# Four small reorderings in a four-layer graph kernel: fetch order, row copies, and VectorE's place in the unit

## The chip, the cores and the metric

The kernel runs on one NeuronCore of a Trainium2 chip. The metric is device time in microseconds (us) of one launch, the median of three runs. The profile is of one further execution, and its span (first to last instruction) is a little shorter than that execution's time.

## The reference, cut to what matters

There are 64 graphs of 256 nodes with 256 features, and one sparse adjacency matrix `adj` (256 x 256, self loops included) that all graphs share. Layers 0, 1 and 3 are the same function with different weights; layer 2 is an attention layer.

```python
def gnn(h, A):                                   # layers 0, 1 and 3
    pre_u = einsum('bud,dk->buk', h, W1[:d]); pre_v = einsum('bvd,dk->bvk', h, W1[d:])
    hidden = relu(pre_u[:, :, None] + pre_v[:, None] + b1)          # for every pair (u, v)
    S = sigmoid(einsum('buvk,ko->buvo', hidden, W2)[..., 0] + b2)   # one score for every pair
    a = einsum('buv,bud->bvd', S * A, h)
    m = einsum('uv,bud->bvd', A, h) * h
    return beta1 * h + beta2 * (a @ Wa + ba) + beta3 * (m @ Wm + bm)
def attention(x, A):                             # layer 2
    f = x @ W1.T; f1 = f @ W2 + b2
    c = softmax(leaky_relu(f1[:, :, None] + f1[:, None, :]) + A)
    return c @ f + bias2 + x
```

Only pairs with an edge need a score, because S is multiplied by A.

## The kernel before, in words

**Edges instead of pairs.** Once, before the loop, the kernel sorts the edges into 16 tiles of 128 edges and one rest tile of 64 edges (for two graphs it fills 128 partitions). A tile lies between 64 nodes u and 64 nodes v. The score of an edge needs row u of pre_u plus row v of pre_v for that edge. Two graphs are worked on at once, so a gathered tile holds 128 edges x 2 graphs x 256 features.

**Two ways of gathering rows.** Eight tiles (`FAST`) are made on TensorE: ScalarE copies rows of `pu` and `pv` into `pre` (`rows_u` copies two tiles at a time, `rows_v` one), and a matmul with a one-hot matrix `pick` spreads them to edges in PSUM (tile `ga`). The other eight (`FETCHED`) and the rest tile are fetched by DMA: SyncE writes `pu` and `pv` to DRAM tables (`tableu`, `tablev`, one write for each half m of the nodes), and GpSimd issues two indirect DMAs for each tile, the first a **copying** fetch from `tableu`, the second an **adding** fetch from `tablev` that accumulates on the first. `FETCHES` is the order of these, as pairs (tile, 0 for copying or 1 for adding); tile -1 is the rest tile `left`. The adding fetch of a tile must wait until its copying fetch has landed. The order of all fetches on GpSimd's queue is fixed by `issue_after(fetches[-1])`. `fetch(st, AHEAD)` issues the first six as soon as the first half of the tables has been handed to SyncE; those read only that half. In two of the six kinds of units two tiles more are fetched and two fewer are made (`FETCHES_MORE`).

**Scores.** For each gathered tile and graph VectorE does one fused relu, multiply and sum (`rated`, output `junk`, sum in a column of `raw`). When the columns of the first half (`EARLY`: rest tile, self loops, tiles with m = 0) are there, `rated_all(EARLY, 0)` makes ScalarE take the tanh (`val`) and VectorE four products (`rm`), and `early` starts the matrix `sa` = S * A from the rest tile and the diagonal (matmuls ps<-ro,guo, then four `sa` operations on VectorE). `rated_all(LATE, 1)` does the same for m = 1 at the end of the unit. `spread` then turns `rm` into `sa` with 32 small matmuls (ps<-rm,gu), the first sixteen with the EARLY `rm`, the other sixteen with the LATE one.

**Units.** Two streams, a and b, each take two graphs at a time, and sixteen such pairs pass through each. A unit is one call of `beside(heavy, light, placed)`: the heavy part is the scores of one stream, the light part what the other stream does between its scores and its next ones: `spread` and `finish` of the layer before, attention where it comes, `before` of the next layer (pre_u, pre_v, tables, first row copies) and the matmuls adj x h. The light part is a generator, and what it yields, (p, f), says how many steps of made tiles and of fetched tiles are traced at that place. Those numbers are `STEPS` and `beside` (a dict of the same name inside `before`). `halfway` mixes `finish` of the last layer with `before` of the next pair's layer 0. One **round** of six units serves two graphs of each stream:

| unit | heavy: scores of | light: the other stream's work | `placed` |
|---|---|---|---|
| U1 | a, layer 0 | b: end of the last layer, then `before` of layer 0 | no |
| U2 | b, layer 0 | a: end of layer 0, `before` of layer 1 | yes |
| U3 | a, layer 1 | b: end of layer 0, `before` of layer 1 | yes |
| U4 | b, layer 1 (more fetched tiles) | a: end of layer 1, attention, `before` of the last layer | no |
| U5 | a, last layer (more fetched tiles) | b: end of layer 1, attention, `before` of the last layer | no |
| U6 | b, last layer | a: end of the last layer, then `before` of layer 0 | no |

So the fetches that serve the scores of U2 are started near the end of U1, and so on: each unit has its own **fetch stream**.

**Who sets the order.** A scheduler orders each engine's instructions; `tc.issue_after(x)` fixes that what is inside comes after x on x's engine. With `placed`, `stay` puts the scores of fetched tiles, the diagonal's scores and the EARLY tanh behind what was traced last on their engine, so that VectorE meets them where the program has them; EARLY is then done as soon as four made tiles are traced and the first four fetched tiles and the rest tile are scored. Without it all made tiles are traced first, EARLY comes near the end, and the scheduler is free. Nearly every instruction is recorded under line 79 (the wrapper that remembers the last one), fetches under line 824, table writes under 677.

Of the kernel before, what the change touches and what calls it, by code (L numbers as in the profile page):

```python
# [17 lines left out]
GNN = ("L0_gnn_", "L1_gnn_", "L3_gnn_")  # L18
LAST = GNN[2]
# [18 lines left out]

FETCHES = [(0, 0), (1, 0), (2, 0), (0, 1), (3, 0), (1, 1)]
FETCHES += [(-1, 0), (2, 1), (4, 0), (3, 1), (-1, 1), (5, 0), (6, 0), (4, 1), (7, 0), (5, 1), (6, 1), (7, 1)]  # L40
FETCHES_MORE = FETCHES[:-2] + [(8, 0), (6, 1), (9, 0), (7, 1), (8, 1), (9, 1)]

AHEAD = 6

STEPS = {
    GNN[0]: [(1, 1), (1, 1), (0, 1), (1, 0), (0, 1), (2, 1)],
    GNN[1]: [0, 0, 0, (0, 1), (0, 1), 1],
    LAST: [1, 1, (0, 1), (1, 1), (0, 1), (2, 1)],
}

VEC = {}
# [11 lines left out]
def blk(c):  # L63
    return slice(c * P, (c + 1) * P)
# [37 lines left out]
def adj_seq_kernel(ctx: ExitStack, tc: tile.TileContext, a: dict, out: bass.AP):  # L102
# [15 lines left out]
    tensor, vector, scalar = Noting(nc.tensor), Noting(nc.vector), Noting(nc.scalar)  # L118
# [383 lines left out]
    def few(stack):  # L502
# [139 lines left out]
        def more(st, l):  # L642

            return (st["side"], l) in (("a", LAST), ("b", GNN[1]))

        def before(st, l):

            hT = st["hT"]
            pu = one.tile([P, 2, 2, D], FP, tag="pu" + st["side"], name="pu")
            pv = one.tile([P, 2, 2, D], FP, tag="pv" + st["side"], name="pv")  # L650
            pre = one.tile([P, len(FAST), 2 * D], FP, tag="pre" + st["side"], name="pre")
            order = [(m, g) for m in range(2) for g in range(2)]
            if l == LAST:
                order = [(m, g) for g in range(2) for m in range(2)]

            beside = {LAST: [0, (0, 1), (0, 1), (0, 1)], GNN[1]: [0] + [(0, 1)] * 3, GNN[0]: [0, 0, (0, 2), (0, 1)]}[l]
            beside = dict(zip(order, beside))
            st["tables"] = [
                tables.tile([N, 2 * D], FP, tag="table" + t + st["side"], name="table" + t) for t in "uv"
            ]  # L660

            st["pu"], st["pv"], st["pre"] = pu, pv, pre
            if l != GNN[1]:
                st["own"] = one.tile([P, 2, 2, D], FP, tag="own", name="own")
            t = one.tile([P, FIRST, 2, D], FP, tag="fetched" + st["side"], name="fetched")
            st["fetched"] = [t[:, f] for f in range(FIRST)]
            for m, g in order:
                if l == LAST and (m, g) == (1, 0):
                    st["flip"](1)
                t = psum()  # L670
                for c in range(2):
                    mm(out=t, lhsT=hT[:, c, g, blk(m)], rhs=w1[l][:, c], start=c == 0, stop=c == 1)
                scalar.copy(pu[:, m, g, :], t[:, 0, :])
                vector.tensor_tensor(pv[:, m, g, :], t[:, 1, :], b1row[l], ALU.add)
                if g == 1:
                    for rows, x in zip(st["tables"], (pu, pv)):
                        nc.sync.dma_start(out=rows[blk(m)], in_=flat(x)[:, m])
                    if m == 0:
                        st["fetches"] = list(FETCHES_MORE if more(st, l) else FETCHES)

                        if numbered:
                            fetch(st, AHEAD)
                if l != GNN[1]:
                    vector.tensor_tensor(st["own"][:, m, g, :], t[:, 0, :], pv[:, m, g, :], ALU.add)
                if g == 1:
                    if m == 0:
                        rows_u(st, 0, 2, 0, 0)
                    rows_v(st, 4 - 4 * m, 2, 0)
                yield beside[(m, g)]
                if l == GNN[1] and (m, g) == (0, 1):  # L690
                    st["turn"](0)
                    yield 0, 1
                    st["turn"](1)
                    yield 0
            yield REST_OF_IT

            yield from mixed(st, l, later if past else None, (0,) if more(st, l) else (0, 1))

        def scores(st, l, placed):
# [3 lines left out]


            stay = behind if placed else lambda engine: nullcontext()
            pre = st["pre"]
            raw = wk.tile([P, LATE.stop], FP, tag="raw", name="raw")
            val = wk.tile([P, LATE.stop], FP, tag="val", name="val")
# [21 lines left out]
            fetched = st["fetched"]  # L730
            fetch(st, len(FETCHES_MORE))

            def tile_scores(t, k, m, i):
                col = BLOCKS + 16 * m + 4 * k + i
                both(t, col, col + 8)
# [18 lines left out]
            def itself(m):  # L754

                with stay(vector):
                    if l == GNN[1]:
                        vector.tensor_tensor(*(flat(t)[:, m] for t in (own, st["pu"], st["pv"])), ALU.add)
                    both(own[:, m], DIAGONAL + 2 * m, DIAGONAL + 2 * m + 1)

            def made():
                for n, (k, m, i) in enumerate(fast):
                    t = ga.tile([P, 2, D], FP, tag="ga", name="ga")
                    with stay(tensor):
                        mm(out=t, lhsT=pick[:, k, 4 * m + i, :], rhs=pre[:, n], start=True, stop=True)
                    tile_scores(t, k, m, i)
                    if 2 * n + 2 < len(fast):

                        with tc.issue_after(past[-1]) if past else nullcontext():
                            rows_u(st, 2 * n + 2, 2, *FAST[2 * n + 2][:2])  # L770
                            if n != 1:
                                rows_v(st, 2 * n + 2, 2, FAST[2 * n + 2][0])
                    if n in (1, 2) and not placed:
                        itself(n - 1)
                    count.append(n)
                    yield
                    if n == 2 and more(st, l):
                        yield from mixed(st, l, None, (1,), ga)

            def got(made):  # L780
                for f, block in enumerate(blocks):
                    if f == FIRST:
                        if placed:
                            while len(count) < 4:
                                next(made)
                        else:
                            for _ in made:
                                yield
                        with stay(vector):
                            rated(left, REST)  # L790
                        rated_all(EARLY, 0)
                        yield
                        if placed:
                            early(st)
                            yield
                    if f < 2 and placed:
                        itself(f)
                    with stay(vector):
                        tile_scores(fetched[f], *block)
                    if f == FIRST + 1 and not placed:  # L800
                        early(st)
                    yield
# [27 lines left out]
        def rows_u(st, f, n, k, m):  # L830

            h = halves[k]
            scalar.copy(
                st["pre"][h, f : f + n],
                st["pu"][h, m].rearrange("p g d -> p (g d)").unsqueeze(1).to_broadcast([64, n, 2 * D]),
            )

        def rows_v(st, f, n, k):

            for n in range(f, f + n):  # L840
                i = FAST[n][2]
                scalar.copy(
                    st["pre"][halves[1 - k], n], st["pv"][halves[i % 2], i // 2].rearrange("p g d -> p (g d)")
                )
# [32 lines left out]
        def after(st, l):  # L877
            yield 1
            yield from spread(st, l)
            yield from finish(st, l)  # L880

        def stream(side, starts):

            sts = [{"b": b, "side": side} for b in starts]
            load(sts[0])
            short = [before(sts[0], GNN[0])]
            for i, st in enumerate(sts):
                yield short, (st, GNN[0]), False
                yield [after(st, GNN[0]), before(st, GNN[1])], (st, GNN[1]), True
                yield [after(st, GNN[1]), attention(st), before(st, GNN[2])], (st, GNN[2]), False  # L890
                short = [after(st, GNN[2])]
                if i + 1 < len(sts):
                    load(sts[i + 1])
                    short = [halfway(after(st, GNN[2]), 4, before(sts[i + 1], GNN[0]), 2)]
            yield short, None, False
# [29 lines left out]
        past, numbered, fetches, later = [], [], [], []  # L925
# [119 lines left out]
```

## Time and profile before

| | us |
|---|---|
| median of three runs | 3469.57 (3468.32 to 3470.26) |
| the profiled execution's own time | 3468.32 |
| its span | 3466.6 |
| TensorE busy | 3361.7 (97%) |
| VectorE busy | 2639.6 (76%) |
| GpSimd busy | 2416.1 (70%) |
| ScalarE busy | 1557.2 (45%) |
| granted TensorE clock, mean | 0.991 |

A busy TensorE is not a TensorE at its peak, because matmuls overlap and their ends are modelled: a stall inside a group shows as a longer interval from one start to the next. One round takes about 210 us, and the sixteen rounds are alike, so stalls are read from the timeline of one round. A GpSimd row is the issue of a fetch, not its transfer. "Idle" in front of a row names what ended the wait.

### The profile page before, as it was taken

The page shows a single profiled execution, that of the slowest core. Times are in us where ns is not written, and L with a number is a line of the kernel's source. Part 1 is how long each engine was busy: PE and PEld are TensorE (multiplying, and loading weights), DVE is VectorE, ACT ScalarE, POOL GpSimd, SP SyncE. Part 2 cuts the span into 40 slices and gives each one's busy share as a digit, 9 for nine tenths or more (in the row PEclk, how much of TensorE's full clock was granted, in tenths as well). Part 3 has the DMA queues.
Part 4 walks back from the last instruction along what each step waited for, and adds up shares of the span by engine and source line. Part 5 has one row for each costly group of instructions (what it writes and reads, how often), then busy time and mean ns, then how long its engine had stood idle before and what let it go on. Part 6 is the DMA issues. An engine that isn't in the chain of part 4 may idle for free.

```text
span 3466.6 us, 48384 instructions
## 1 busy us (share of the span) xinstructions
PE 3361.7 (97%) x14200; PEld 2067.6 (60%) x14200; DVE 2639.6 (76%) x10523; ACT 1557.2 (45%) x2833; POOL 2416.1 (70%) x1882
## 2 busy tenths in 40 slices
PE   6999999999999999999999999999999999999998
PEld 3566565565656566565665656656565665656655
DVE  5777787777777777777777877777777777777776
ACT  2444444444444444444444444444444444444442
POOL 3767777677767767677677776777767676776765
PEclk7999999999999999999999999999999999999999
DMA  5788787877878778787787877878787787877875
GB/s 148 164 185 188 166 207 164 193 176 178 197 168 196 179 178 186 176 196 171 178 188 165 197 170 187 183 170 205 167 196 173 178 197 165 193 179 175 190 162 129
DMA packets 289070, 620.81 MB, mean 179 GB/s; under 512 B 39072, under 2 KB 56352, under 8 KB 288800
## 3 DMA queue, kind: packets, MB, share of 16 engines
q0 software_dynamic: 204800, 461.49, 65.2%
q1 hardware_dynamic: 82416, 154.96, 12.8%
q8 instruction: 115, 1.88, 0.2%
q10 hardware_dynamic: 1584, 1.20, 0.1%
q14 instruction: 155, 1.27, 0.1%
HBM read 500.06 MB, written 117.44 MB: 178 GB/s over the span
## 4 chain that ended last, share of the span: by engine, by line
PE 68%; POOL 9%; DMA 7%; issue 7%; DVE 6%; ACT 3%; ACTq 0%; POOLq 0%; DVEq 0%
PE ps L79 52%; PE ga L79 16%; POOL fetched L824 8%; DMA fetched<-tablev,ids_v 4%; DVE junk L79 3%; ACT pre L79 2%; DMA fetched<-tableu,ids_u 2%; DVE rm L79 1%; DMA tableu<-pu 1%; POOL left L824 1%; DVE sa L79 1%; ACT val L79 1%; ACT pu L79 1%; DVE own L79 0%; DVE pv L79 0%
## 5 line engine op out<-in xcount | busy, mean ns | idle before, releaser
L824 POOL DMA_INDIRECT fetched<-tablev,ids_v x832 | 1317.3, 1583 | 381.1 <-issue 257.0
L824 POOL DMA_INDIRECT fetched<-tableu,ids_u x832 | 843.7, 1014 | 547.1 <-DMA tableu<-pu 286.7
L79 DVE SCALAR_TENSOR_TENSOR junk<-fetched,L_gnn_w2row 128x256 f32<-128x256 f32 x1664 | 643.0, 419 | 171.3 <-DMA fetched<-tablev,ids_v 167.3
L79 PE MATMUL ga<-pre,pick 128*128 128x512 f32 x1408 | 723.5, 609 | 37.0 <-ACT pre L79 27.4
L79 PE MATMUL ps<-L_gnn_w,hT 128*128 128x512 f32 x1536 | 708.0, 598 | 5.7 <-DMA hT<-in_xT_dram 5.7
L79 DVE SCALAR_TENSOR_TENSOR junk<-ga,L_gnn_w2row 128x256 f32<-128x256 f32 x1408 | 538.3, 419 | 103.7 <-PE ga L79 92.2
L79 PEld LDWEIGHTS ps<-L_gnn_w,hT 128*128 128x128 f32 x1536 | 280.6, 191 | 323.7 <-issue 300.2
L79 ACT COPY pre<-pv 64x512 f32<-64x512 f32 x704 | 434.0, 616 | 72.6 <-DVE pv L79 49.3
L79 PE MATMUL ps<-sa,h 128*128 128x256 f32 x1536 | 363.7, 382 | 13.2 <-DVE sa L79 8.9
L79 PEld LDWEIGHTS ps<-sa,h 128*128 128x128 f32 x1536 | 292.5, 191 | 126.0 <-issue 68.5
L79 ACT COPY pre<-pu 64x1024 f32<-64x1024 f32 x352 | 361.6, 1044 | 8.0 <-DVE ids_v L79 0.6
L79 PEld LDWEIGHTS ga<-pre,pick 128*128 128x128 f32 x1408 | 249.2, 191 | 184.4 <-issue 91.3
L79 ACT COPY pu<-ps 128x256 f32<-128x256 f32 x384 | 142.8, 372 | 481.3 <-PE ps L79 430.8
L79 ACT ACTIVATE hb<-hT,L_gnn_zbias,scas 128x512 f32<-128x512 f32 x128 | 97.3, 807 | 477.9 <-DVE hT L79 354.5
L79 DVE TENSOR_TENSOR rm<-gva,val 128x256 f32<-128x256 f32 x768 | 280.1, 420 | 33.1 <-ACT val L79 24.2
L79 PE MATMUL ps<-adj,h 128*128 128x256 f32 x1280 | 297.2, 384 | 4.0 <-issue 4.0
L79 PEld LDWEIGHTS ps<-adj,h 128*128 128x128 f32 x1280 | 242.1, 191 | 73.7 <-issue 40.3
L79 DVE TENSOR_TENSOR pv<-ps,L_gnn_b1row 128x256 f32<-128x256 f32 x384 | 161.7, 421 | 134.5 <-ACT pu L79 125.6
L79 PEld LDWEIGHTS ps<-rm,gu 128*64 128x64 f32 x3072 | 175.1, 138 | 135.2 <-issue 50.3
L79 ACT COPY aT<-ps 128x512 f32<-128x512 f32 x192 | 112.4, 585 | 315.9 <-PE ps L79 284.6
L79 PE MATMUL ps<-rm,gu 128*64 128x128 f32 x3072 | 218.7, 281 | 23.0 <-DVE rm L79 22.6
L79 PE MATMUL ps<-aT,L_gnn_Wa 128*128 128x512 f32 x512 | 240.6, 592 | 0.0
(149 smaller groups left out, 4211.8 us busy)
## 6 DMA issues: line engine op xcount, KB each, us to landing
tableu<-pu SPq DMA_DIRECT2D x192, 256.0 KB
tablev<-pv SPq DMA_DIRECT2D x192, 256.0 KB
hT<-in_xT_dram SPq DMA_DIRECT2D x32, 512.0 KB
h<-in_x_dram SPq DMA_DIRECT2D x64, 256.0 KB
out_dram<-h SPq DMA_DIRECT2D x64, 256.0 KB
fetched<-tableu,ids_u POOLq DMA_INDIRECT x832
fetched<-tablev,ids_v POOLq DMA_INDIRECT x832
L_gnn_w<-in_L_gnn_W_dram SPq DMA_DIRECT2D x6, 256.0 KB
```

What stands on the lines that cost most here:

```text
L79: self.last = getattr(self.engine, op)(*a, **k)
L824: this = nc.gpsimd.indirect_dma_start(out=to, out_offset=None, in_=rows, in_offset=bass.IndirectOffsetOnAxis(ap=ids, axis=0), compute_op=( ...
```

## The change

It does five things.

1. `APART` is a second order of fetches, in which a copying fetch follows another copying fetch only at the very start. It is used in the streams of U2, U3, U4 and U5 (in the last two through `FETCHES_MORE`). The streams of U6 and U1 (`tight`) keep `FETCHES`.
2. The row copies of later made tiles (`rows_u`, `rows_v` from tile 2 on) are queued on ScalarE behind the last row copy of `before`, which fills tiles 0 and 1.
3. U1 and U6 become `placed` (from the second round on), which moves EARLY, `early` and the rest tile's score to the middle of the unit and fixes VectorE's order there. The diagonal's scores (`itself`) stay where they were in all units, through `diagonal_later`.
4. `STEPS[LAST]` moves one fetched tile's step from the first z matmuls to one step earlier.
5. The dict `beside` of layer 0 spreads four fetched steps evenly over the four blocks of `before`.

```diff
-FETCHES_MORE = FETCHES[:-2] + [(8, 0), (6, 1), (9, 0), (7, 1), (8, 1), (9, 1)]
+APART = [(0, 0), (1, 0), (0, 1), (2, 0), (1, 1), (3, 0)]
+APART += [(-1, 0), (2, 1), (4, 0), (3, 1), (5, 0), (-1, 1), (6, 0), (4, 1), (7, 0), (5, 1), (6, 1), (7, 1)]
+FETCHES_MORE = APART[:-2] + [(8, 0), (6, 1), (9, 0), (7, 1), (8, 1), (9, 1)]
...
-    LAST: [1, 1, (0, 1), (1, 1), (0, 1), (2, 1)],
+    LAST: [1, (1, 1), 0, (1, 1), (0, 1), (2, 1)],
...
-            beside = {LAST: [0, (0, 1), (0, 1), (0, 1)], GNN[1]: [0] + [(0, 1)] * 3, GNN[0]: [0, 0, (0, 2), (0, 1)]}[l]
+            beside = {LAST: [0, (0, 1), (0, 1), (0, 1)], GNN[1]: [0] + [(0, 1)] * 3, GNN[0]: [(0, 1)] * 4}[l]
...
-                        st["fetches"] = list(FETCHES_MORE if more(st, l) else FETCHES)
+                        tight = (st["side"], l) in (("b", LAST), ("a", GNN[0]))
+                        st["fetches"] = list(FETCHES_MORE if more(st, l) else FETCHES if tight else APART)
...
                     rows_v(st, 4 - 4 * m, 2, 0)
+                    st["rows"] = scalar.last.ins
...
+            diagonal_later = placed and (st["side"], l) in (("b", GNN[0]), ("a", GNN[1]))
...
-                        with tc.issue_after(past[-1]) if past else nullcontext():
+                        with tc.issue_after(past[-1]) if past else nullcontext(), tc.issue_after(st["rows"]):
...
-                    if n in (1, 2) and not placed:
+                    if n in (1, 2) and not diagonal_later:
...
-                    if f < 2 and placed:
+                    if f < 2 and diagonal_later:
...
-                yield short, (st, GNN[0]), False
+                yield short, (st, GNN[0]), i > 0
```

The order before, for comparison:

```python
FETCHES = [(0, 0), (1, 0), (2, 0), (0, 1), (3, 0), (1, 1)]
FETCHES += [(-1, 0), (2, 1), (4, 0), (3, 1), (-1, 1), (5, 0), (6, 0), (4, 1), (7, 0), (5, 1), (6, 1), (7, 1)]
```

## The prediction

> **What bounds the kernel now.** I read the page first: busy shares, then its costliest groups.
>
> ```profile
> PE 3361.7 (97%) x14200; PEld 2067.6 (60%) x14200; DVE 2639.6 (76%) x10523; ACT 1557.2 (45%) x2833; POOL 2416.1 (70%) x1882
> ...
> L824 POOL DMA_INDIRECT fetched<-tablev,ids_v x832 | 1317.3, 1583 | 381.1 <-issue 257.0
> L824 POOL DMA_INDIRECT fetched<-tableu,ids_u x832 | 843.7, 1014 | 547.1 <-DMA tableu<-pu 286.7
> ```
>
> TensorE is the bound, and the change takes no matmul away: only TensorE's stalls can be won or lost. 97% busy hides some, since a stalled matmul counts as busy, so I took intervals between starts in the trace. A run of 32 ps<-rm,gu takes 1.90 us unstalled; 2 ga<-pre,pick take 0.86. Against such values a round of about 210.7 us holds some 9 us of stalls, nearly all at the six unit boundaries. The timeline shows them. U4's end:
>
> ```profile
> 1253.56 1.04 ACT L79 COPY pre<-pu 64x1024 f32<-64x1024 f32 x1
> ...
> 1254.25 1.09 DVE L79 TENSOR_TENSOR rm<-gva,val 128x256 f32<-128x256 f32 x3
> 1254.63 2.52 ACT L79 COPY pre<-pv 64x512 f32<-64x512 f32 x4
> ...
> 1255.30 1.12 PE L79 MATMUL ga<-pre,pick 128*128 128x512 f32 x2 [1.01 <-ACT pre L79]
> ```
>
> ScalarE copies rows of tiles 2 and 3 (1.04 us) before the last rows of tile 0, and TensorE, in order, waits 1.01 us for tile 0. U1's end:
>
> ```profile
> 1360.35 0.31 ACT L79 ACTIVATE val<-raw,L_gnn_halfb 128x16 f32<-128x16 f32 x1 [2.71 <-DVE junk L79]
> ...
> 1360.94 1.49 DVE L79 TENSOR_TENSOR rm<-gva,val 128x256 f32<-128x256 f32 x4 [0.62 <-ACT val L79]
> ...
> 1362.15 1.42 PE L79 MATMUL ps<-rm,gu 128*64 128x128 f32 x16 [0.55 <-DVE rm L79]
> ```
>
> Here the LATE `rm` comes last: the group of 32 took 2.88 us in nearly every round, 0.98 over. U6's end is alike (0.61 over). At U3's end the wait reaches back to a fetch:
>
> ```profile
> 791.90 0.42 DVE L79 SCALAR_TENSOR_TENSOR junk<-fetched,L_gnn_w2row 128x256 f32<-128x256 f32 x1 [1.28 <-DMA fetched<-tablev,ids_v]
> ...
> 794.78 1.33 PE L79 MATMUL ps<-rm,gu 128*64 128x128 f32 x16 [1.30 <-DVE rm L79]
> ```
>
> And GpSimd's queue at the start of a stream (here U4's):
>
> ```profile
> 1420.77 0.98 POOL L824 DMA_INDIRECT fetched<-tableu,ids_u  x1 [3.17 <-DMA tableu<-pu]
> 1422.05 1.13 POOL L824 DMA_INDIRECT fetched<-tableu,ids_u  x1 [0.30 <-issue]
> 1423.49 0.96 POOL L824 DMA_INDIRECT fetched<-tableu,ids_u  x1 [0.30 <-issue]
> 1425.84 1.56 POOL L824 DMA_INDIRECT fetched<-tablev,ids_v  x1 [1.38 <-issue]
> ```
>
> Three copying fetches at 0.98 + 0.30 = 1.28 us each, then the first adding fetch, 5.07 us after the stream's start. Over 95 streams that distance was 3.9 to 7.1 us, and three issues need 3.84: almost always the queue already waits, after the third copying fetch, for the first to land. The first fetch's gap says what started the stream: 3 to 6 us of waiting for tableu in the streams of U3 to U6, but 0.30 in those of U1 and U2, in every round: there GpSimd goes from stream to stream without a pause.
>
> **What the Trainium skill says.** "Perfetto Trace Analysis", section "DMA Instruction — SWDGE (GPSIMD)": a fetch's row on GpSimd ends with its descriptors, not with its data. The trace agrees: rows of 1.55 us, but the packets of a stream's last adding fetch end 4.4 to 7.1 us after its issue. "DMA: Bandwidth & Descriptors", section "Why a DMA increments its semaphore by 16 and not by 1": data is there when all engines have counted. In the stream at 1324.08 the counts of the first copying fetch came from 1328.38 to 1329.90, and the adding fetch went at 1330.16. The same page, section "Two DMAs through the same engine are not ordered": within a queue of an engine descriptors start in order. So a later copying fetch shouldn't delay an earlier one's landing; the ends that the trace has for the three, staggered (1329.90, 1330.52, 1331.15), agree.
>
> **The change, part by part** (per round).
>
> *Row copies ahead.* Queued behind tiles 0 and 1, the 1.04 us copy no longer precedes tile 0. At U4's end ga could start at about 1254.3 instead of 1255.30; the second half of ps<-rm,gu then needs the `rm` that ends at 1255.34, against 1256.35 now. Gain **0.9**. U5's end has the same order (TensorE 0.48 over), but what follows is paced by the fetch chain below, so I count it there. The other boundaries have the right order already. ScalarE does the same copies at 45% busy.
>
> *U1 and U6 placed, with the new steps.* Moved to mid-unit: the rest tile's score (0.42), four `rm` (1.43) and four `sa` (1.64), 3.5 us of VectorE, plus ScalarE's tanh, add and `ro`, and the eight ps<-ro,guo matmuls. VectorE has holes there (2.17 and 1.29 us beside the last layer's z), and ScalarE idles 5.8 to 8.5 us. No DMA is moved. The end of U1 gets free of 3.5 us. What is late next is the last adding fetch: by the packet times VectorE began on it 1.62 us after it landed in U1 (mean; median 1.70; 0.41 is the least seen) and 1.35 in U6. TensorE could save 0.98 + 0.61 + 0.48 = 2.07, but the streams of U6 and U1 run back to back on GpSimd, so the sum can't exceed U1's slack: 1.62 − 0.41 = 1.2 mean, and 1.0 with each round cut at the smaller of both. Gain **1.0**. New waits: fixed scores of fetched tiles stand on VectorE ahead of pv and of the last layer's sums. By packet times their data lands 0.3 to 2 us ahead in U6 and more in U1: I count nothing; if late, pv, then the tables, then the next stream wait up to 0.5.
>
> *Fetches apart.* U2 to U5. The second order issues two copying fetches, then an adding one that waits for the first. If that lands when it did, the adding fetch starts at the same moment; the third copying fetch, until now issued inside the wait, comes after it. Everything from the rest tile on is 0.98 + 0.30 = **1.28 later** in each of the four streams, the last adding fetch too. The later swap (5 before the rest tile's add) removes no wait, but lands the rest tile 2.56 later; its score in U2 and U3 has about as much slack. Where it counts: U5 has about 2.2 spare: nothing. U2 has 0.2 to 4, and its successor's stream waits 3 to 5 for its table: up to 0.3. U3 has about none: VectorE starts within 0.6 of the landing, so its end slips the full 1.28. U4 has none either, but its stream starts before U3's slip and TensorE, 0.9 late by then, hides most. Also queued behind tile 3's score in U2 and U3 is `hT` of layer 0, with about 1 us before a matmul needs it. Bounds: from −0.5 (spread copies land sooner, and the adds behind them find less backlog; the trace of before can't show it, and the order within a queue speaks against it) to 3.8 (U2, U3 and U4 each in full). I take **1.28**.
>
> Sum: −0.9 − 1.0 + 1.28 = −0.6 to −0.7 a round; in some rounds U4's end gains the whole 1.0. With −0.7 and 15.5 rounds (the first isn't placed): **−11 us**. The profiled execution took 3468.3 (span 3466.6, 1.7 around it), 1.2 below the median of the runs; from 3468.3 that is 3457, against the median 3458.
>
> **Rivals.**
> - *Spreading is free.* Landings come sooner by what the order costs; then −1.9 × 15.5 = −29: about **3439**, and at −3 a round (U6's and U1's stalls gone in full) 3423. For it: TensorE's stalls of that size are in every round. Against: the order within a queue.
> - *All is given back.* VectorE's waits for tile 3 in U2 and U3 (already in 5 and 10 of 16 rounds) grow by 1.28 and push `hT`, and U2's end slips 0.3: +0.5, so −0.2 a round: **3467**, no measurable change (0.2%, 7 us, is about what can be told).
> - *The fetch streams become the bound: slower.* U2's end slips too, since U1's gain has used up its slack, and U3's and U4's slips add because their scores start as soon as data lands: 3 × 1.28 = 3.8 against 1.9 won, +1.2 to +1.9 a round: +19 to +29, about **3490**. It decides once U2's spare is under 1.28. For it: U1's and U2's streams have no pause. Against: U2's end never stalled before.
> - *It does not do what it says*: the scheduler, free in U4 to U6 outside the placed parts, answers new fetch times with another order that brings back a late row copy: within 7 us of **3470**.
>
> **How the numbers follow.** Forecast 0.32, spreading free 0.24, given back 0.12, no effect 0.06, fetch streams the bound 0.26. Those give faster 0.54, same 0.16, slower 0.30 (edges of the cases spill over). The forecast's own range is 3445 to 3462. To leave at most 2 in 10 out it must reach to both sides: 3422 to 3488.
>
> **What would show it.** Right: ga at U4's end without its wait for pre; a run of 32 ps<-rm,gu near 1.9 at U1's end; the first adding fetch third in its stream at an unchanged distance from the start, and the third copying fetch behind it; longer waits of VectorE for the last adds in U3 and U4. Wrong: an adding fetch that starts 2.6 to 3.5 us after its stream's start (copies land sooner), stalls at U2's end, or at a row copy still out of order.

## The result, and the profile after

In 12 runs each the changed kernel took 3471.06 us (median; 3462.44 to 3481.75) and the kernel before 3468.28 us (3461.14 to 3475.41). The ratio is 1.0008, with a 95% interval from 0.9996 to 1.002: no change that a measurement can tell. The profiled execution is one of these runs and took 3464.07 us, 7 us under their median (span 3462.3, clock 0.991 as before).

The page of the changed kernel, the lines that answer to those shown of before (helpers are at L82 now, fetches at L831; "|" sets apart busy time and mean ns from idle time ahead and what ended it):

```profile
PE 3356.7 (97%) x14200; PEld 2073.3 (60%) x14200; DVE 2651.4 (77%) x10523; ACT 1555.3 (45%) x2833; POOL 2415.5 (70%) x1882
...
L831 POOL DMA_INDIRECT fetched<-tablev,ids_v x832 | 1322.7, 1590 | 449.5 <-DMA fetched<-tableu,ids_u 229.7
L831 POOL DMA_INDIRECT fetched<-tableu,ids_u x832 | 841.9, 1012 | 473.6 <-DMA tableu<-pu 223.9
```

TensorE's share is what it was. What moved is GpSimd's idle time: waits for a copying fetch to land now lead the adding fetches' row, and waits for a new table (286.7 us before) have fallen to 223.9: streams that are longer leave less of a pause between them. A stream of U5 shows the new order in the timeline (U2's to U4's begin alike):

```profile
1468.21 0.98 POOL L831 DMA_INDIRECT fetched<-tableu,ids_u  x1 [4.65 <-DMA tableu<-pu]
1469.49 1.07 POOL L831 DMA_INDIRECT fetched<-tableu,ids_u  x1 [0.30 <-issue]
1473.04 1.56 POOL L831 DMA_INDIRECT fetched<-tablev,ids_v  x1 [2.48 <-DMA fetched<-tableu,ids_u]
1474.91 1.04 POOL L831 DMA_INDIRECT fetched<-tableu,ids_u  x1 [0.30 <-issue]
```

The adding fetch is third, 4.83 us after the start, and the third copying fetch comes behind it. Over all rounds this distance moved by no more than 0.4 us in the means of the streams of U2 to U5, so the first landing came about when it did. (Behind the start the new order still has one pair of neighbours: the copying fetches of tile 3 and of the rest tile.) U4's end, in another timeline window:

```profile
1465.97 1.04 ACT L82 COPY pre<-pu 64x1024 f32<-64x1024 f32 x1
...
1469.29 1.26 ACT L82 COPY pre<-pv 64x512 f32<-64x512 f32 x2
...
1469.96 1.13 PE L82 MATMUL ga<-pre,pick 128*128 128x512 f32 x2 [0.41 <-ACT pre L82]
1470.46 1.04 ACT L82 COPY pre<-pu 64x1024 f32<-64x1024 f32 x1
```

The large copy now follows the last rows that TensorE needs; ga's waits for pre at this place sum to 13.0 us over 16 rounds, from 23.9. U1's end:

```profile
1577.34 0.31 ACT L82 ACTIVATE val<-raw,L_gnn_halfb 128x16 f32<-128x16 f32 x1 [1.27 <-DVE junk L82]
...
1577.93 1.43 DVE L82 TENSOR_TENSOR rm<-gva,val 128x256 f32<-128x256 f32 x4 [0.62 <-ACT val L82]
1578.15 2.35 PE L82 MATMUL ps<-rm,gu 128*64 128x128 f32 x32
```

The 32 matmuls take about 2.3 us, from 2.88; 1.90 would be no stall. U3's end still hangs on the last fetch:

```profile
1428.72 0.42 DVE L82 SCALAR_TENSOR_TENSOR junk<-fetched,L_gnn_w2row 128x256 f32<-128x256 f32 x1 [0.44 <-DMA fetched<-tablev,ids_v]
...
1431.60 1.33 PE L82 MATMUL ps<-rm,gu 128*64 128x128 f32 x16 [0.34 <-DVE rm L82]
```

So the aimed-at stalls at the ends of U4 and U1 did shrink. The time came back in U6. Its end, in one round:

```profile
1332.33 0.42 DVE L82 SCALAR_TENSOR_TENSOR junk<-fetched,L_gnn_w2row 128x256 f32<-128x256 f32 x1 [1.26 <-DMA fetched<-tablev,ids_v]
1333.14 0.31 ACT L82 ACTIVATE val<-raw,L_gnn_halfb 128x16 f32<-128x16 f32 x1 [3.53 <-DVE junk L82]
...
1333.73 1.43 DVE L82 TENSOR_TENSOR rm<-gva,val 128x256 f32<-128x256 f32 x4 [0.63 <-ACT val L82]
1334.98 1.33 PE L82 MATMUL ps<-rm,gu 128*64 128x128 f32 x16 [3.02 <-DVE rm L82]
```

Read it upward: TensorE stands 3.02 us for rm, rm for val, val for the score of the last fetched tile, and that score for its adding fetch. Not every round is like this. By packet times VectorE begins that score within 0.7 us of the landing in 6 of 14 rounds, as often as before the change. Of the 1.14 us by which U6 is longer in the mean (counted as in the table below), about 0.6 lie in the run of ps<-rm,gu at its end. The other 0.5 lie at its start, where TensorE's ps<-sa,h wait for a sum of VectorE; more on that wait below.

### The profile page after: what moved, and what is told of

It is laid out like the page before. It is cut to its first block, busy times and chain, and to the rows that moved or that the text cites. A ratio compares the mean times of both kernels' runs of the same rounds, so it can differ in the third digit from the quotient of the medians.

```text
span 3462.3 us, 48195 instructions
## 1 busy us (share of the span) xinstructions
PE 3356.7 (97%) x14200; PEld 2073.3 (60%) x14200; DVE 2651.4 (77%) x10523; ACT 1555.3 (45%) x2833; POOL 2415.5 (70%) x1882
## 4 chain that ended last, share of the span: by engine, by line
PE 67%; DMA 11%; POOL 11%; issue 6%; DVE 4%; ACT 2%; ACTq 0%; POOLq 0%; DVEq 0%
PE ps L82 52%; PE ga L82 15%; POOL fetched L831 9%; DMA fetched<-tablev,ids_v 6%; DMA fetched<-tableu,ids_u 3%; DVE junk L82 2%; POOL left L831 1%; DMA tableu<-pu 1%; ACT pre L82 1%; DVE sa L82 1%; DVE own L82 0%; ACT val L82 0%; DVE rm L82 0%; DMA h<-in_x_dram 0%; ACT pu L82 0%
## 5 line engine op out<-in xcount | busy, mean ns | idle before, releaser
L831 POOL DMA_INDIRECT fetched<-tablev,ids_v x832 | 1322.7, 1590 | 449.5 <-DMA fetched<-tableu,ids_u 229.7
L831 POOL DMA_INDIRECT fetched<-tableu,ids_u x832 | 841.9, 1012 | 473.6 <-DMA tableu<-pu 223.9
L82 DVE SCALAR_TENSOR_TENSOR junk<-fetched,L_gnn_w2row 128x256 f32<-128x256 f32 x1664 | 641.3, 419 | 213.5 <-DMA fetched<-tablev,ids_v 208.9
L82 PE MATMUL ga<-pre,pick 128*128 128x512 f32 x1408 | 726.1, 609 | 31.7 <-ACT pre L82 19.6
L82 PE MATMUL ps<-L_gnn_w,hT 128*128 128x512 f32 x1536 | 706.7, 598 | 5.6 <-DMA hT<-in_xT_dram 5.6
L82 DVE SCALAR_TENSOR_TENSOR junk<-ga,L_gnn_w2row 128x256 f32<-128x256 f32 x1408 | 536.2, 419 | 92.3 <-PE ga L82 74.8
L82 PEld LDWEIGHTS ps<-L_gnn_w,hT 128*128 128x128 f32 x1536 | 280.0, 191 | 322.7 <-issue 294.3
L82 ACT COPY pre<-pv 64x512 f32<-64x512 f32 x704 | 434.1, 617 | 75.7 <-DVE pv L82 59.3
L82 PE MATMUL ps<-sa,h 128*128 128x256 f32 x1536 | 362.2, 381 | 9.3 <-DVE sa L82 8.5
L82 PEld LDWEIGHTS ps<-sa,h 128*128 128x128 f32 x1536 | 292.6, 191 | 121.1 <-issue 63.8
L82 ACT COPY pre<-pu 64x1024 f32<-64x1024 f32 x352 | 361.5, 1044 | 6.6
L82 PEld LDWEIGHTS ga<-pre,pick 128*128 128x128 f32 x1408 | 248.6, 191 | 176.7 <-issue 101.3
L82 ACT COPY pu<-ps 128x256 f32<-128x256 f32 x384 | 142.8, 372 | 470.7 <-PE ps L82 441.1
L82 DVE TENSOR_TENSOR rm<-gva,val 128x256 f32<-128x256 f32 x768 | 278.0, 420 | 61.4 <-ACT val L82 52.4
L82 PE MATMUL ps<-adj,h 128*128 128x256 f32 x1280 | 295.9, 383 | 5.6 <-issue 4.5
L82 PEld LDWEIGHTS ps<-adj,h 128*128 128x128 f32 x1280 | 245.4, 192 | 81.2 <-issue 42.1
L82 ACT ACTIVATE hb<-hT,L_gnn_zbias,scas 128x512 f32<-128x512 f32 x128 | 97.3, 806 | 416.2 <-DVE hT L82 366.0
L82 PEld LDWEIGHTS ps<-rm,gu 128*64 128x64 f32 x3072 | 178.4, 138 | 131.0 <-issue 74.3
L82 DVE TENSOR_TENSOR pv<-ps,L_gnn_b1row 128x256 f32<-128x256 f32 x384 | 161.7, 421 | 118.5 <-ACT pu L82 108.0
L82 ACT COPY aT<-ps 128x512 f32<-128x512 f32 x192 | 112.4, 585 | 305.2 <-PE ps L82 266.7
L82 PE MATMUL ps<-rm,gu 128*64 128x128 f32 x3072 | 218.4, 280 | 31.3 <-DVE rm L82 27.7
L82 PE MATMUL ps<-mT,L_gnn_Wm 128*128 128x512 f32 x512 | 240.7, 592 | 0.0
```

The costliest lines, as they stand in the source:

```text
L82: self.last = getattr(self.engine, op)(*a, **k)
L831: this = nc.gpsimd.indirect_dma_start(out=to, out_offset=None, in_=rows, in_offset=bass.IndirectOffsetOnAxis(ap=ids, axis=0), compute_op=( ...
```

## The experiments

Twelve kernels ran in three lots of four. Each lot had a chip of its own, and the kernel before ran beside it there: 3467.64, 3467.17 and 3463.26 us. Each ratio of the twelve is against the kernel before on the same chip. This table holds each part alone, in pairs, and together. "Rows" are the row copies ahead; "placed" is U1 and U6 placed, with the later diagonal, the new steps and `beside`; "order" is the spread order in the streams of U2 to U5. A column gives the mean time (us) from the end of one unit's last run of ps<-rm,gu to the next unit's, over the rounds of one profiled execution behind the first; the sum is a round. In kernels with the placed parts TensorE runs two ga<-pre,pick in U1 instead of U6; their 0.86 is booked in U6 here throughout.

| kernel | U1 | U2 | U3 | U4 | U5 | U6 | round | ratio to before [95%] |
|---|---|---|---|---|---|---|---|---|
| before | 31.28 | 31.69 | 31.97 | 41.40 | 42.23 | 32.91 | 211.5 | |
| rows | 31.30 | 31.86 | 32.00 | 40.30 | 41.84 | 33.83 | 211.1 | 1.0002 [0.9987, 1.0016] |
| placed | 30.43 | 31.73 | 31.82 | 40.78 | 42.34 | 33.09 | 210.2 | 0.9986 [0.9974, 0.9997] |
| rows, placed | 30.84 | 31.69 | 31.90 | 40.41 | 42.18 | 34.30 | 211.3 | 0.9992 [0.9982, 1.0002] |
| order | 31.29 | 32.01 | 33.07 | 41.23 | 43.16 | 33.08 | 213.8 | 1.0089 [1.0071, 1.0107] |
| rows, order | 31.47 | 32.03 | 32.99 | 40.53 | 42.76 | 33.49 | 213.3 | 1.0078 [1.0061, 1.0094] |
| placed, order | 30.48 | 31.94 | 32.47 | 40.82 | 42.74 | 32.96 | 211.4 | 1.0076 [1.0061, 1.009] |
| all (the change) | 30.59 | 31.69 | 32.17 | 40.25 | 42.28 | 34.05 | 211.0 | 1.0008 [0.9996, 1.002] |

A profiled execution is one sample, up to 14 us off its kernel's median (that of placed and order is the one 14 below); the ratios decide on totals, the columns on places. The columns also hold the wait for VectorE's sum: at the start of U6 it takes 0.3 us before, 0.8 in the changed kernel, 0.1 to 0.4 in the first lot and nothing in the last lot (here rows with order and placed with order). In U3 it takes 0.3 before and at most 0.1 in the others, so U3's slips are some 0.2 to 0.3 larger than the columns say. In the expectations a unit's "stream" is its fetches.

**Order taken back, order alone, rows alone, placed alone.**

```
e1_order_back, on the changed kernel:
-APART = [(0, 0), (1, 0), (0, 1), (2, 0), (1, 1), (3, 0)]
-APART += ...
+APART = FETCHES
e2_apart_only, on the kernel before: + APART, FETCHES_MORE made from it, and
+    st["fetches"] = list(FETCHES_MORE if more(st, l) else FETCHES if tight else APART)
e3_rows_only, on the kernel before:
+    st["rows"] = scalar.last.ins
+    with tc.issue_after(past[-1]) if past else nullcontext(), tc.issue_after(st["rows"]):
e4_placed_only, on the kernel before:
+    yield short, (st, GNN[0]), i > 0
     (with diagonal_later, STEPS[LAST] and beside of layer 0)
```

> The changed kernel with the old fetch order in all streams; row copies ahead and placed U1 and U6 stay. Theory A (the new order gives back what the other parts win): 24 to 38 us below the kernel before (ratio 0.989 to 0.993); fetch streams of U3, U4, U5 as long as before (27.4, 34.6, 35.0 us), U4's end keeps its gain of about 1.1 us a round. Theory B (the order is neutral; the gain of the placed part is swallowed by the fetch streams of U6 and U1, which run without a pause): within 7 us of the changed kernel.

> The kernel before with only the new fetch order in the streams of U2 to U5. Theory A: 20 to 35 us slower (ratio 1.006 to 1.010), the streams 0.8 to 1.9 us longer, new waits of VectorE for fetched tiles before U5's end. Theory B: within 7 us of the kernel before.

> The kernel before with only the row copies of tiles 0 and 1 ahead of the later ones. Theory A: 10 to 18 us faster (0.7 to 1.1 us a round, at U4's end: ga no longer waits 1.0 us for pre). Theory B: the same 10 to 18 us, since both count this part as a gain. If it is within 5 us, the stall at U4's end only moved to the next wait and both are wrong here.

> The kernel before with only U1 and U6 placed and the two lists of steps. Theory A: 8 to 16 us faster, won at U1's end (ps<-rm,gu there 0.6 to 1.0 us shorter). Theory B: within 7 us, or slower, U6's end losing what U1's end wins because both wait for the last adding fetch.

They took 3465.45, 3498.88, 3466.16 and 3461.64 us. Neither theory stood. The order is not neutral: alone it costs 31 us, as theory A had it. But rows, placed, and both without the order win 5 us at most (by the ratios), so what was missing was not what the order gave back. Theory B's half held here: gains were swallowed. For rows alone the third case held, the stall that only moved to the next wait. On all the engines but GpSimd the order alone leaves the instructions as in the kernel before, and taking it back leaves them as in the changed kernel, so the scheduler has no part in what the order costs.

Where they were swallowed is in the trace. U6's end in the kernel with rows alone, timeline:

```profile
1329.20 0.42 DVE L79 SCALAR_TENSOR_TENSOR junk<-fetched,L_gnn_w2row 128x256 f32<-128x256 f32 x1 [1.12 <-DMA fetched<-tablev,ids_v]
...
1331.79 1.42 PE L79 MATMUL ps<-rm,gu 128*64 128x128 f32 x16 [1.84 <-DVE rm L79]
```

By packet times VectorE begins U6's last fetched tile within 0.7 us of its landing in 12 of 14 rounds here, in 6 of 14 before. And the landing hardly moves (packet times give it to some 0.3 us). Counted from U3's end (means): TensorE reaches U5's end at 83.63 us before, 82.14 with rows, 82.60 with rows and placed, 82.53 in the changed kernel; U6's last adding fetch lands at 110.97, 111.19, 111.30 and 110.92. TensorE is 1.0 to 1.5 us ahead at U5's end and runs into the same landing, with rows alone in most rounds, in the changed kernel in 6 of 14. No run moved this landing by itself: that it is the cap is read from these traces. What holds it back is where the streams start: U5's begins some 5 us ahead of U4's end, on a table written before the stall that was removed. With rows alone TensorE is 1.10 us sooner at U4's end, U5's stream only 0.45 (from 36.37 to 35.92 after U3's end); VectorE then waits 0.66 longer for U5's first fetched tile and 0.21 longer for the second, and U6's stream starts 0.25 sooner (78.08 to 77.83), which the last fetch's own time takes back.

**Which streams make the order dear, and do shorter streams help.** Four copying fetches first would use the wait for the first landing and end every stream earlier.

```
e5_four_first, on the kernel before (all streams); e7 on placed alone, e8 on rows and placed:
-FETCHES = [(0, 0), (1, 0), (2, 0), (0, 1), (3, 0), (1, 1)]
+FETCHES = [(0, 0), (1, 0), (2, 0), (3, 0), (0, 1), (1, 1)]
e6_apart_u2_u3, on order alone:
-FETCHES_MORE = APART[:-2] + ...
+FETCHES_MORE = FETCHES[:-2] + ...
```

> The kernel before with one edit: every stream begins with four copying fetches instead of three and an adding one, so the fourth copying fetch is issued inside the wait for the first landing. The order of the instructions on the other four engines is that of the kernel before. Theory C (the fetch streams pace the round: the last adding fetch of U6, U1 and U3 sets the end of these units): streams of U1 and U2 1.3 us shorter, of the others 0.5 to 1.0; TensorE's stalls at the ends of U6, U1 and U3 shrink by what the streams lose; 1.0 to 2.5 us a round, 16 to 40 us faster. Theory D (the streams are not the bound; order costs only where it delays a score that stands ahead of a VectorE queue, as in U5): within 7 us of the kernel before. Rival E (four copies at once get in each other's way, the first lands later): slower by up to 15 us.

> The kernel before with the order APART in the streams of U2 and U3 alone; U4 and U5 keep their order. Orders of the other four engines as before. In U2 to U5 together the order cost 31 us, by unit 0.32 in U2, 1.1 in U3, -0.17 in U4, 0.93 in U5, 0.17 in U6 a round. Theory C (a stream that is 1.3 to 2.3 us longer costs where its last landing ends the unit: U3): 1.2 to 1.5 us a round, 19 to 24 us slower. Theory D (it costs in U5, at the eighth fetched score ahead of the attention chain): 0 to 8 us slower.

> The placed parts alone (U1 and U6 placed, diagonal later, new steps, new beside) on the kernel before, and four copying fetches first in every stream; orders of the four other engines as in the run with the placed parts alone, which was 5 us faster than before. Theory C: shorter streams let the placed U6 and U1 end without waiting for the last landing: 20 to 45 us faster than before. Theory D: 0 to 12 us faster, as without the shorter streams.

> The changed kernel with its order of fetches replaced in all six units by the old order with four copying fetches first; orders of the other four engines as in the changed kernel. Theory C: rows ahead and placed work both won TensorE time that was lost again to the last landing of U6 and U1; with streams 1 us shorter that is kept: 25 to 45 us faster than before. Theory D: within 7 us of the run with the old order (2 us faster than before).

The order in U2 and U3 alone: 3475.37 us, ratio 1.0026 [1.0017, 1.0036], some 9 us of the 31. Its profile has U2 at +0.27, U3 at +0.87 and U4 at −0.84: what U3 slips, U4 mostly makes good. The other 22 us, by subtraction, come with the order in U4 and U5. With the order alone U5 loses most of its time in TensorE's run of ps<-adj,h: 4.76 us to the next start, against 3.98 before (means). VectorE's wait for U5's eighth fetched tile, 0.01 us before, is 0.40 with the order alone and 1.13 in the changed kernel (in 14 of 16 rounds). What stands behind that tile, in the changed kernel's timeline:

```profile
1507.54 0.42 DVE L82 SCALAR_TENSOR_TENSOR junk<-fetched,L_gnn_w2row 128x256 f32<-128x256 f32 x1 [2.73 <-DMA fetched<-tablev,ids_v]
...
1507.89 0.42 DVE L82 TENSOR_TENSOR own<-ps,pv 128x256 f32<-128x256 f32 x1
...
1508.45 3.69 PE L82 MATMUL ps<-adj,h 128*128 128x256 f32 x16 [0.40 <-DVE own L82]
...
1513.56 1.12 PE L82 MATMUL ga<-pre,pick 128*128 128x512 f32 x2 [1.41 <-ACT pre L82]
```

The score waits 2.73 us; own, behind it on VectorE, lets TensorE stand 0.40, and pv, later still, delays the rows of pre, for which ga stands 1.41. The length of this wait does not tell what it costs: in the changed kernel it is longer, yet ps<-adj,h takes 4.09 us only, because rows ahead shorten the same place (3.60 with rows alone). So the chain is seen, and its share of the 22 us is not measured.

Four copies first was worse than any theory had it: 3522.31 us (1.0147 [1.0123, 1.0171]) on the kernel before, 3513.92 (1.0136 [1.0116, 1.0157]) on placed, 3523.15 (1.0177 [1.0152, 1.0201]) on both. Yet it did what it was to do: the streams of U1 to U4 are 1.1, 1.5, 0.2 and 0.9 us shorter, VectorE's waits for fetched tiles fell from 167.3 to 69.9 us, and U1, U2 and U3 took 31.07, 31.69 and 31.34. The loss is one wait that no theory named: TensorE's ps<-sa,h wait for VectorE's sum. Counted from start to start, these runs are 5.8 us a round longer than without a stall, against 0.9 in the kernel before. Over 16 rounds the difference is 78 us, more than the 55 lost, so some of it came back at other places. One group row each; first the kernel before, then four first:

```profile
L79 PE MATMUL ps<-sa,h 128*128 128x256 f32 x1536 | 363.7, 382 | 13.2 <-DVE sa L79 8.9 <-issue 4.3
```

```profile
L79 PE MATMUL ps<-sa,h 128*128 128x256 f32 x1536 | 385.1, 394 | 65.0 <-DVE sa L79 61.8 <-issue 2.3
```

One instance, at U3's end, in the timeline of four first:

```profile
2737.16 1.09 PE L79 MATMUL ps<-rm,gu 128*64 128x128 f32 x16
...
2738.40 1.57 POOL L824 DMA_INDIRECT fetched<-tablev,ids_v  x1 [0.30 <-issue]
...
2740.27 1.54 POOL L824 DMA_INDIRECT fetched<-tablev,ids_v  x1 [0.30 <-issue]
2741.82 0.69 DVE L79 TENSOR_TENSOR sa<-sa,ps 128x512 f32<-128x512 f32 x1 [3.32 <-remote]
...
2742.56 0.79 PE L79 MATMUL ps<-sa,h 128*128 128x256 f32 x1 [2.82 <-DVE sa L79]
```

VectorE's sum sa<-sa,ps needs TensorE's run of ps<-rm,gu, whose record ends at 2738.25, and waits for nothing else in the program; it begins at 2741.82. The view names no releaser ("remote"). But the trace also holds the times at which semaphores were updated, though not all of them, and there TensorE's updates stand at 2741.80, 2741.84 and 2741.88: its signal came late, and VectorE began with it. The same holds for 493 of the 498 sums that were over 0.3 us late in the ten traces outside the last lot: an update by TensorE stands within 0.06 us ahead of the start. "Late" is counted here from the later of two ends, that of the matmuls that the sum needs and that of VectorE's instruction before it. The second sum of a unit is 2.2 us late (mean) at U3's end and 2.1 at U4's, against 0.4 and 0.2 in the kernel before.

**A pause put back, the two missing pairs, and four first where it doesn't meet a sum.**

```
e9_four_wait, on the kernel before:
+FETCHES = [(0, 0), (1, 0), (2, 0), (3, 0), (1, 1), (0, 1)]
e10_rows_apart: rows and order;  e11_placed_apart: placed and order
e12_placed_four_u1_u2, on placed alone:
+FOUR = [(0, 0), (1, 0), (2, 0), (3, 0), (0, 1), (1, 1)] + FETCHES[6:]
+    st["fetches"] = list(FETCHES_MORE if more(st, l) else FOUR if l == GNN[0] else FETCHES)
```

> As the run with four copying fetches first on the kernel before, with one swap: the first adding fetch is that of tile 1, which waits for the second copying fetch to land, then that of tile 0. In the run with four first the adds followed the copies without a pause (0.30 us) and VectorE's sum sa<-sa,ps began 1.5 to 2.2 us after TensorE's last ps<-rm,gu row at the ends of U3, U4 and U5 (0.2 to 0.8 in the kernel before); TensorE's idle time before ps<-sa,h went from 13 to 65 us. Theory P (the pause on GpSimd is what lets that sum start): a wait of 0.6 to 1.4 us is back ahead of the first add, the idle time before ps<-sa,h falls under 30 us, and the time is 3455 to 3485. Theory F (four copying fetches in flight do it): still 40 to 60 us slower than before, idle time before ps<-sa,h over 50 us.

> The kernel before with the row copies ahead and the order APART in the streams of U2 to U5, nothing placed. Order alone cost 31 us, rows alone 0. Theory G (the order costs through late row copies: VectorE's waits for fetched tiles push pv, pv pushes the copies, and TensorE's ga waits for them; rows ahead take that away): 0 to 8 us slower than before. Theory H (parts add up; the placement absorbs the cost): 25 to 31 us slower than before.

> The kernel before with the placed parts and the order APART in the streams of U2 to U5, no row copies ahead. Theory G (rows ahead absorb the order's cost): 15 to 28 us slower than before, ga's waits for pre as long as with the order alone (48 us). Theory H (the placement absorbs it): within 7 us of before.

> The placed parts on the kernel before, and four copying fetches first in the streams of U1 and U2 alone; these start some 9 us before the end of the unit ahead of them, so their first adds do not meet its sums sa<-sa,ps. If the streams of U6, U1 and U2, which run back to back, still pace U1's end there: 3 to 12 us faster than the placed parts alone (3450 to 3458). If nothing hangs on these streams any more: within 4 us of the placed parts alone (3462). If four copies in a row are harmful wherever they stand: 10 us or more slower than that.

With the adding fetch of tile 1 first the kernel took 3469.67 us, 1.0017 [1.0007, 1.0026], inside theory P's range. GpSimd waits 0.8 to 2.0 us ahead of the first add (unit means), and the row shown above of the other two reads here:

```profile
L79 PE MATMUL ps<-sa,h 128*128 128x256 f32 x1536 | 358.3, 380 | 0.0
```

This run alone does not show that the pause did it. It ran on the last lot's chip, and there no sum is late in any of the four kernels: all 768 begin within 0.1 us. Two places with the same order of fetches, and no pause ahead of the first add, at U5's end; first the kernel before, then the last kernel of this lot:

```profile
2359.41 1.58 POOL L824 DMA_INDIRECT fetched<-tablev,ids_v  x1 [0.30 <-issue]
...
2362.68 0.69 DVE L79 TENSOR_TENSOR sa<-sa,ps 128x512 f32<-128x512 f32 x1 [2.29 <-PE ga L79]
```

```profile
1087.65 1.56 POOL L826 DMA_INDIRECT fetched<-tablev,ids_v  x1 [0.30 <-issue]
...
1088.96 0.69 DVE L80 TENSOR_TENSOR sa<-sa,ps 128x512 f32<-128x512 f32 x1 [0.19 <-PE ps L80]
```

What the pause does is better read from rounds of one kernel that have it and rounds that do not. Seven of the ten other traces have two or three copying fetches first. At the ends of their units U3 to U5 GpSimd waited less than 0.45 us ahead of the next stream's first add in 48 cases, and the unit's two sums together were 2.0 us late (mean); it waited 0.9 us or more in 229 cases, and they were 0.1 late. So on those chips the sums come late where the pause is missing, and four copies in flight (theory F) are not needed for it. On the last lot's chip the pause was as short in 28 cases, and the sums were 0.1 late. What is different there the runs do not tell. Its traces keep a quarter to two fifths more of the updates that landing DMAs make than the other ten, so the recording itself may have a part in the wait. Four first in all streams was not run on that chip.

Rows with order took 3492.47 us and placed with order 3489.45. Theory G (rows absorb the order's cost) and theory H (placement does) each hold in one of these runs only by half: neither part alone takes the cost away, 0.76% and 0.90% are left, and only both bring it to 0.16%. That it takes both is measured (the rows with order and placed with order ran on the last chip, where the kernel before is 4 us faster, 0.12%, too little to make this difference); why, these runs don't settle. The table shows where, as far as one execution each can: U3's slip, 1.1 with order and with rows and order, 0.5 with placed and order, is 0.2 in the changed kernel, and U5's is 0.05 instead of 0.5 to 0.9.

The last kernel took 3454.12 us, 0.9979 [0.9968, 0.999]. It beats the kernel before and the changed one (whose interval starts at 0.9996); against placed alone (0.9986) the difference is too small to tell. Its time lies in the range of the first case, but that range was made from times on another chip; by the ratios the first and the second case can't be told apart. The third, that four copies in a row are harmful wherever they stand, is out on this chip. In its profile the idle time ahead of ps<-sa,h is 0.0, as in this whole lot, U2's waits for fetched tiles are gone, U3 takes 31.49 instead of 31.82, and U6's last landing sits at 111.33 us after U3's end, as in the kernels above: all 14 rounds begin its score within 0.7 us of it.

## Why the prediction was right, and where its steps failed

The total lies inside a range (3422 to 3488) that was wide enough for nearly all the rivals, near the two that foresaw no change, "all is given back" (3467) and "it does not do what it says" (3470). The second of these is out: the scheduler did not answer the new fetch times with another order. The likeliest case (3458, 3445 to 3462) was too low by 13 us. That the total fell inside is in part luck, because two errors of opposite sign met: of 29 us forecast as gains some 3 were kept, and of 20 us forecast as the order's price about 5 were paid. The mechanisms were found one by one, but they don't add up as the sum had them.

- **Rows ahead, 0.9 a round.** Right in its place: U4 takes 1.10 less with rows alone. The failed term is what is kept of it: U6 takes 0.92 more, because its last landing stays where it was, and the kernel is no faster.
- **Placed, 1.0 a round.** U1's end gained 0.85 of the 0.98 aimed at. U6's 0.61 failed: U6 takes 0.18 more with the placed parts alone, 1.14 more in the changed kernel (0.5 of it the sum's wait at its start). The prediction took U6's slack, 1.35 us between landing and score, as fixed; it is there only as long as TensorE and VectorE come late. Some 5 us of the 15.5 remain.
- **U6 and U1 back to back** was seen as a cap and set at U1's slack. U1 kept slack (VectorE starts 1.84 us after the landing). By the traces the cap is U6's landing, with rows alone in 12 of 14 rounds, in the changed kernel in 6.
- **Fetches apart, 1.28 a round, 20 us.** The step "the adding fetch starts at the same moment, the rest is later" held: the distance from the stream's start changed by −0.4 to +0.1 us in U2 to U5 (means; by −0.3 to +0.7 with the order alone). The streams of U2 to U5 grew by 0.8, 1.4, 1.9 and 0.9. The price alone was 31 us, inside the bounds to 3.8 a round, and about 5 in company. "U3 slips the full 1.28 and U4 hides most" is what order in U2 and U3 shows (+0.87, −0.84).
- **"U5 has about 2.2 spare: nothing"** was wrong: an average slack at U5's end says nothing of its eighth fetched tile, which stands ahead of own and pv.
- **A stall that is not in its list.** Late sums held up the runs of ps<-sa,h for 0.9 us a round in the kernel before. The prediction looked at the unit boundaries and did not name this wait, which a change of the fetch order can lengthen or take away.
- **All given back** was reached another way than that rival's: the waits for tile 3 grew in U3 (0.42 to 1.10) and in U2 (0.20 to 0.42), but U2's end did not slip.
- **The Trainium skill.** "DMA: Bandwidth & Descriptors", section "Two DMAs through the same engine are not ordered", has descriptors of one queue start in order. The prediction drew from it that a later copying fetch does not hold up an earlier one's landing. The runs agree: with one copying fetch fewer behind it, the adding fetch that waits for the first landing started at most 0.4 us sooner (the distances just given).

## What to carry to other kernels

A stall removed at the end of a stage is won only if what the next stages wait for moves too: measure the landing of each stage's last transfer from one fixed point, and ask whether the write that starts its stream lies ahead of the stall or behind it. Slack read from one trace belongs to that trace's pace and can't be spent twice. Parts of a change that share such a ring of waits have to be run alone, in pairs and together, as here one part cost 31 us alone and 5 in company. And an experiment that is to show a cause has to stand beside its control on the same chip: the run that put the pause back had a chip on which the wait was missing anyway.

## What the runs showed of the hardware

Unexpected was a late signal from TensorE. Where GpSimd issued adding fetches without a pause, TensorE's semaphore update for a finished run of small matmuls was recorded up to 3.5 us behind the end of that run's record (four first on the kernel before), and VectorE's sum began only with it; with a pause of 0.9 us or more the two sums of a unit were 0.1 us late together. On the third chip no sum was over 0.1 us late, with a pause or without. Four first cost 55 us on the second chip. Whether the matmuls' results or only the signal were late is not told, because the ends of matmul records are modelled.

The Trainium skill, "SBUF — State Buffer", section "Who interferes with whom", names a port that VectorE and GpSimd share, but says that a VectorE instruction with at most one input in SBUF, outside its two-port modes, does not contend. This sum has one input in SBUF and one in PSUM, and the traces agree: it did not stand in contention but waited for its signal. What held the signal up stays open.
